# Placing small TensorE work later in a hand-planned instruction order: convolutional attention and correlation layers on one core

## The chip, the cores and the metric

The kernel runs on one NeuronCore of a Trainium2 chip. The metric is the device time in microseconds (us) of one execution. The core has five engines with a queue each: TensorE (PE in the profile; its weight loads are PEld), VectorE (DVE), ScalarE (ACT), GpSimd (POOL) and SyncE (SP), which here issues nearly all DMA transfers. SBUF is the on-chip memory, PSUM the memory that TensorE writes to.

## What is computed

Eight images of 768 channels and 32 x 32 pixels (1024 tokens) pass two residual layers. A group norm (32 groups) stands ahead of each. The first layer is an attention with 12 heads of 64 channels whose scores are outer products of variances; the second multiplies the pixels by a matrix, together with 28 local correlations of the pixel-normalized features.

```python
# layer 0: x = x + L0(gn(x))
q, k, v = qkv                                   # q is not used
var_v = var(v, axis=-1, ddof=1); var_k = var(k, axis=-1, ddof=1)
attn = softmax(var_v @ var_k.T * hd ** -0.5)    # 1024 x 1024 for each head
out = (attn @ v) @ W_proj.T + b_proj
# layer 1: x = x + L1(gn(x))
feat_n = feature / norm(feature, over channels)
corr[r, c] = sum over channels of shift(feat_n, r, c) * feat_n   # 28 shifts
out = concat(feature, corr) @ conv_w.T + conv_b
```

## The kernel before, in words

**Tiles.** An image is held as 128 partitions x 6 channel blocks x 1024 tokens in float32. A pair is two heads, so there are 6 pairs; a half is three pairs. Token tiles `t` are 128 tokens, 8 to an image; `hf` is a half of 512 tokens.

**Layer 0.** `Layer0.group(half, t)` multiplies a token tile by the key or the value weights of a half (six matmuls into one PSUM buffer of `mm`, which has 3). VectorE takes the statistics of each head from PSUM (line 307), values are copied to SBUF by ScalarE or VectorE, and after the eighth tile `head_m2` works out the squared deviations `m2`. For values, `spread` then transposes `m2` on TensorE (`to_rows`, line 279, tile `ptv`) and writes it as rows to DRAM. For keys, the maximum over all tokens is subtracted first (`nk`, with GpSimd's all-reduce, line 334), and the transpose is `ptk`. `Pair.rows` (line 382) reads a row back broadcast over 128 partitions: `bc` for the exponentials, `bk` for the denominators.

**Attention.** For each pair and each key tile ScalarE makes two tiles of exponentials (`exponentials`, line 392), and `products` multiplies them with the values (line 416, tile `av`). A step is one key tile. The denominators are a second pass of ScalarE over exponentials whose outputs are thrown away (`junk`, line 402) but whose sums are kept. After a pair's eighth denominator tile, `invert` takes the reciprocal on VectorE (line 425), `spread` transposes it on TensorE (line 431, tile `it`), writes it to DRAM (`di`) and reads it back broadcast (`rd`), and `finish` multiplies `av` by `rd` on VectorE (line 445). There are 6 buffers of exponentials (three steps), 2 of `av` and one of `rd`.

**Projection and layer 1.** `Project` multiplies the pairs' outputs by `wp` and adds to `x1` (lines 516, 525), where the image was loaded a second time. `Corr.gram(t)` multiplies a token tile with its neighbours (line 542) and VectorE picks 13 diagonals from the PSUM tile (line 550). After four grams `scale` works out the norms, `columns` applies them, `to_dram` transposes (line 577, tile `ct`) and writes rows; after eight, `gather` reads shifted rows for one half of the pixels and `product` multiplies them to `cs` (line 605). `Conv.group(n)` is the main product of an output block (line 630). If `cs` is ready, one more matmul adds the correlations (line 620, `cv<-cs`); if not, the unit leaves a late unit behind, `Conv.late`: the matmul `cc` into another PSUM buffer and an addition on VectorE (line 647). When all parts of a half are there, the half is stored; when all of both are, the next image's `x1` is loaded 12 us later.

**What sets the order.** Nothing is scheduled by the compiler: each engine executes its instructions in the order in which this program emits them. The program keeps a model clock (`Clock`). A unit of TensorE work is emitted and the clock is advanced by the unit's assumed time: 3.9 us for a key or value group, 2.4 for a gram, 5.2 for a conv, 0.9 for a late product. `later.after(us, job)` puts a job on a list; it is emitted when the clock passes its due time, which may be in the middle of a unit's or step's time, and so behind that unit's instructions. A second model time, `clock.act`, follows ScalarE: `EXP` and `SUM` are its assumed times for one exponential and one denominator tile, `STEP_US` TensorE's for one step of `products`. `work_off` alternates: if `can_run` says that ScalarE is far enough, four steps are emitted (a run; 12 runs to an image), otherwise the first unit of the list `rest` whose gate is ready (`pick`). If no more than `TAIL` us of other work is left, it is held back until the attention is over. The list of image `b` holds the second half of its values, layer 1 of image `b - 1` and all keys of image `b + 1`. The last value group also starts the load of the next image, and 14 us later `first_norm`: twelve statistics on VectorE, then `means` (TensorE tile `pma`), `spreads` (`pva`) and `apply`.

Of the kernel before, what the change touches and what calls it, by code (L numbers as in the profile page):

```python
# [32 lines left out]
HH = NH // 2  # L33
STEPS = 4
AHEAD = 3
TAIL = 8.0
EXP, SUM, STEP_US = 1.12, 1.32, 1.78


def windows(ap, *dims):  # L40
# [48 lines left out]
def two_layers(ctx, tc, x, wkv, wproj, bproj, wconv, wcorr, bconv, out):  # L89
# [26 lines left out]
    clock = Clock()  # L116
    later = clock
    ready = set()
# [7 lines left out]
    def small(name):  # L126
        return smp.tile([P, 512], F32, tag="sm", name=name)
# [5 lines left out]
    def load(pl, tag, b):  # L133
        t = pl.tile([P, J, N], F32, tag=tag, name=f"{tag}{b}")
        for j in range(J):
            nc.sync.dma_start(out=t[:, j, :], in_=xv[b, :, j, :])
        return t
# [30 lines left out]
    xn = load(xnpool, "xn", 0)  # L168
# [43 lines left out]
    def gn_tile(name):  # L212
        return st.tile([P, 2 * J, 6], F32, tag="bn", bufs=2, name=name)

    def gn_stats(bn, t, j, hf):
        nc.vector.bn_stats(out=bn[:, 2 * j + hf, :], in_=t[:, j, hf * HF : (hf + 1) * HF])  # L216
# [30 lines left out]
            for j in range(J):  # L247
                nc.vector.tensor_scalar(to[:, j, :], src[:, j, :], self.mean, self.rstd, ALU.subtract, ALU.mult)  # L248

    def first_norm(b, xn):  # L250

        bn = gn_tile(f"bn1_{b}")
        for j in range(J):
            for hf in range(2):
                gn_stats(bn, xn, j, hf)
        norm = Norm(bn, f"a{b}")
        later.after(3.0, norm.means)
        later.after(6.0, norm.spreads)

        def apply():  # L260
            norm.apply(xn, xn)
            ready.add(("xn", b))

        later.after(8.0, apply)


    def head_m2(bn, m2, name):
# [17 lines left out]
    class Layer0:  # L285
# [31 lines left out]
        def to_dram(self, cols, half):  # L317
            to_rows(cols, self.dr[half], f"{self.kind}{self.b}_{half}")
            ready.add((self.kind, self.b, half))

    class Keys(Layer0):
# [7 lines left out]
        def spread(self, half):  # L329
            b, m2 = self.b, self.m2[half]  # L330
            top = st.tile([P, HH], F32, tag="top", name=f"top{b}_{half}")
            nc.vector.tensor_reduce(top, m2.rearrange("p t h -> p h t"), AX.X, ALU.max)
            most = st.tile([P, HH], F32, tag="most", name=f"most{b}_{half}")
            nc.gpsimd.partition_all_reduce(most, top, P, bass_isa.ReduceOp.max)
            nk = st.tile([P, MT, HH], F32, tag="nk", bufs=4, name=f"nk{b}_{half}")
            self.nk.append(nk)

            def scaled():
                for t in range(MT):
                    nc.vector.tensor_tensor(nk[:, t, :], m2[:, t, :], most, ALU.subtract)  # L340
                nc.vector.tensor_scalar(nk, nk, HD ** -0.5 / (HD - 1) ** 2, None, ALU.mult)
                later.after(2.0, lambda: self.to_dram(nk, half))

            later.after(2.0, scaled)

    class Values(Layer0):
# [11 lines left out]
                    nc.vector.tensor_copy(to, at)  # L358

        def spread(self, half):  # L360
            later.after(2.5, lambda: self.to_dram(self.m2[half], half))


    class Pair:
        def __init__(self, b, hp, keys, values, ot):
            half = hp // 3
            self.b, self.hp, self.half, self.vt, self.ot = b, hp, half, values.vt[hp], ot
            self.keys, self.values = keys, values
            self.rows_at = {}
            self.exs = {}  # L370
            self.passes = {"e": 0, "s": 0}

# [37 lines left out]
        def products(self, t):  # L410
            if t == 0:
                self.av = avp.tile([P, 2, HF], F32, tag="av", name=f"av{self.b}_{self.hp}")
            exs = self.exs.pop(t)
            for hf in range(2):
                for e in range(2):
                    nc.tensor.matmul(  # L416
                        self.av[e * HD : (e + 1) * HD, hf, :], lhsT=self.vt[:, t, e, :],
                        rhs=exs[e][:, hf * HF : (hf + 1) * HF], start=t == 0, stop=t == MT - 1,
                    )
            if t == MT - 1:  # L420
                later.after(1.0, self.finish)

        def invert(self):
            self.inv = st.tile([P, 2 * MT], F32, tag="inv", bufs=2, name=f"inv{self.b}_{self.hp}")
            nc.vector.reciprocal(self.inv, self.sums.rearrange("p e t -> p (e t)"))
            later.after(1.5, self.spread)

        def spread(self):
            b, hp = self.b, self.hp
            pt = small(f"it{b}_{hp}")  # L430
            nc.tensor.transpose(pt[0 : 2 * MT, 0:P], self.inv, ident)
            row = work([2 * MT, P], f"ir{b}_{hp}")
            nc.vector.tensor_copy(row, pt[0 : 2 * MT, 0:P])
            dr = dpool.tile([2 * MT, P], F32, tag="inv", name=f"di{b}_{hp}")
            nc.sync.dma_start(out=dr, in_=row)
            self.rd = rdpool.tile([P, N], F32, tag="rd", name=f"rd{b}_{hp}")
            for e in range(2):
                nc.sync.dma_start(
                    out=self.rd[e * HD : (e + 1) * HD, :], in_=windows(dr[e * MT : e * MT + 1, :], (0, HD), (1, N))
                )  # L440

        def finish(self):
            for hf in range(2):
# [87 lines left out]
    class Corr:  # L531
# [25 lines left out]
        def scale(self, hf, dd):  # L557

            b = self.b
            m = st.tile([P, 4], F32, tag="m", name=f"m{b}_{hf}")  # L560
            nc.vector.tensor_scalar(m, dd[:, :, 0], NORM_EPS2, None, ALU.max)
            rn = st.tile([P, 4], F32, tag="rn", name=f"rn{b}_{hf}")
            nc.gpsimd.tensor_tensor(rn, m, neghalf, ALU.pow)

            def columns():
                dn = st.tile([P, 4, NROW], F32, tag="dn", bufs=2, name=f"dn{b}_{hf}")
                nc.vector.tensor_copy(dn[:, :, 0], rn)
                nc.vector.tensor_tensor(dn[:, :, 13], dd[:, :, 0], rn, ALU.mult)
                for q in range(4):
                    nc.vector.scalar_tensor_tensor(  # L570
                        dn[:, q, 1:13], dd[:, q, 1:13], rn[:, q : q + 1], mask_m, ALU.mult, ALU.mult
                    )
                later.after(3.0, lambda: to_dram(dn))

            def to_dram(dn):
                pt = small(f"ct{b}_{hf}")
                nc.tensor.transpose(pt[0 : 4 * NROW, 0:P], dn.rearrange("p q r -> p (q r)"), ident)
                cr = work([4 * NROW, P], f"cr{b}_{hf}")
                nc.vector.tensor_copy(cr, pt[0 : 4 * NROW, 0:P])
                for q in range(4):  # L580
                    at = PAD + hf * HF + q * P
                    nc.sync.dma_start(out=rows[b % 2][:, at : at + P], in_=cr[q * NROW : (q + 1) * NROW, :])
                if hf == 1:
                    self.gather()

            later.after(2.5, columns)
# [88 lines left out]
    def do(unit):  # L675

        more = unit[2]()
        clock.pass_time(unit[0])
        return [more] if more else []

    def pick(rest):
        n = next((n for n, r in enumerate(rest) if r[1] is None or r[1] in ready), None)
        return None if n is None else rest.pop(n)

    def work_off(rest, attention=None):
        while rest or (attention and not attention.over()):
            if attention and not attention.over():
                attention.load_rows()
                clock.feed_act()
                if attention.can_run():  # L690
                    attention.run()
                    continue
                if sum(r[0] for r in rest) <= TAIL:
                    clock.pass_time(0.5)
                    continue
            unit = pick(rest)
            if unit is None:
                clock.pass_time(0.5)
            else:
                rest[:0] = do(unit)  # L700

    first_norm(0, xn)
    clock.settle()
    x1s = [load(x1pool, "x1", 0)]
    keys, values = Keys(0, xn), Values(0, xn)
# [3 lines left out]
    for b in range(NB + 1):  # L709
        rest, attention = [], None  # L710
# [10 lines left out]
        if b + 1 < NB:  # L721

            def next_image(b=b):
                t = load(xnpool, "xn", b + 1)
                next_keys.xn = t
                clock.after(14.0, lambda: first_norm(b + 1, t))

            next_keys = Keys(b + 1, None)
            last = next(n for n, r in enumerate(rest) if n + 1 == MT * (1 + (b == 0)))
            us, gate, unit = rest[last]  # L730
            rest[last] = (us, gate, always(lambda unit=unit: (unit(), next_image())))
            rest += layer0_units(next_keys, (0, 1), ("xn", b + 1))
        work_off(rest, attention)
        if b < NB:
# [14 lines left out]
            norm = Norm(project.bn, f"b{b}")  # L749
# [45 lines left out]
```

## Time and profile before

The median of three runs is 3330.92 us (3329.41 to 3335.73). The profiled execution spans 3330.4 us.

| engine | busy, us | share | instructions |
|---|---|---|---|
| PE | 3011.1 | 90% | 9568 |
| ACT | 1794.3 | 54% | 2497 |
| DVE | 1072.9 | 32% | 4689 |
| POOL | 37.1 | 1% | 73 |

The costliest groups on PE are `av` (734.9 us), the convs (512.1), keys (511.1), values (505.8) and the projection (525.9 in two groups). The mean granted TensorE clock is 0.961 of full speed. Images 1 to 6 take some 400 us each and look alike.

How to read the lines below: a line of the timeline has start, duration, engine, source line, operation, output <- inputs, shapes and count, then in brackets the idle time of the engine before it and what it waited for. A line of the waits has the waiting instruction, what released it, the idle time in all, the number of waits and the longest. Float32 matmuls show as two records each. An idle time of an engine that is not the bottleneck costs nothing.

### The profile page before, as it was taken

To read this page: it belongs to the slowest core of one execution; us is meant where nothing else is said; L and a number is where in the kernel's file an instruction comes from. 1 tells how busy PE (TensorE), PEld (TensorE's weight loads), DVE (VectorE), ACT (ScalarE), POOL (GpSimd) and SP (SyncE) were. 2 spreads that over 40 slices of the span, in tenths; PEclk is the share of its full clock that TensorE was granted. 3 is DMA by queue.
4 is the path that set the end of the run, shared out by engine and by line. 5 is a ranking of instruction groups with operands and counts; after the bars stand their busy time and mean duration, and the time that the engine had idled before them with its cause. 6 is when DMAs were issued, how large, how long until landed. Compare 5 with 4: busy or idle time off the path is not lost.

```text
span 3330.4 us, 28877 instructions
## 1 busy us (share of the span) xinstructions
PE 3011.1 (90%) x9568; PEld 1439.0 (43%) x9568; DVE 1072.9 (32%) x4689; ACT 1794.3 (54%) x2497; POOL 37.1 (1%) x73
## 2 busy tenths in 40 slices
PE   7978798899988998999989999889998899997698
PEld 4433354344543444434444445434454344542244
DVE  3231135312352234422344123441235312342044
ACT  0669326781467805776058740777326782377700
POOL 0000000000000000000000000000000000000000
PEclk9988899999999999999999999999999999999799
DMA  3231113231232213142031411324113231222201
GB/s 134 99 126 56 35 67 112 73 136 36 81 116 84 107 64 118 52 141 76 37 137 44 160 55 54 111 68 155 35 67 112 73 136 35 74 86 86 73 39 42
DMA packets 86606, 282.29 MB, mean 85 GB/s; under 512 B 12702, under 2 KB 15902, under 8 KB 84410
## 3 DMA queue, kind: packets, MB, share of 16 engines
q1 hardware_dynamic: 84730, 275.74, 23.9%
q10 hardware_dynamic: 1728, 4.72, 0.4%
q8 instruction: 75, 1.23, 0.2%
q14 instruction: 73, 0.60, 0.1%
HBM read 253.59 MB, written 26.83 MB: 84 GB/s over the span
## 4 chain that ended last, share of the span: by engine, by line
PE 84%; DVE 5%; ACT 5%; DMA 4%; issue 1%; SPq 1%; POOL 0%; ACTq 0%; DVEq 0%; POOLq 0%
PE av L416 17%; PE k L301 15%; PE v L301 15%; PE pr L516 14%; PE cv L630 14%; PE gr L542 4%; ACT junk L402 3%; PE cc L620 2%; ACT ex L392 2%; DVE bn L216 1%; DMA di<-ir 1%; DMA rd<-di 1%; DVE sc L550 1%; PE cv L620 1%; DVE vbn L307 0%
## 5 line engine op out<-in xcount | busy, mean ns | idle before, releaser
L392 ACT ACTIVATE ex<-bc,nk 128x1024 f32<-128x1024 f32 x768 | 812.3, 1135 | 521.6 <-PE av L416 438.0
L402 ACT ACTIVATE junk<-bk,m2v 128x1024 bf16<-128x1024 f32 x768 | 880.3, 1146 | 38.6 <-DMA bk<-drk 16.8
L416 PE MATMUL av<-ex,v 128*64 128x512 f32 x3072 | 734.9, 627 | 29.6 <-ACT ex L392 29.6
L301 PE MATMUL k<-wk,xn 128*128 128x384 f32 x1536 | 511.1, 492 | 3.7 <-DVE xn L248 1.8
L630 PE MATMUL cv<-f,wc 128*128 128x512 f32 x1152 | 512.1, 594 | 0.0
L301 PE MATMUL v<-wv,xn 128*128 128x384 f32 x1536 | 505.8, 489 | 0.0
L356 ACT COPY v<-v 128x128 f32<-128x128 f32 x192 | 38.6, 274 | 765.9 <-PE v L301 765.9
L416 PEld LDWEIGHTS av<-ex,v 128*64 128x64 f32 x3072 | 224.9, 143 | 478.3 <-issue 413.8
L516 PE MATMUL pr<-v,wp 128*128 128x512 f32 x960 | 427.7, 592 | 0.0
L301 PEld LDWEIGHTS k<-wk,xn 128*128 128x128 f32 x1536 | 291.0, 191 | 229.5 <-issue 34.9
L301 PEld LDWEIGHTS v<-wv,xn 128*128 128x128 f32 x1536 | 290.3, 191 | 204.7 <-issue 12.3
L630 PEld LDWEIGHTS cv<-f,wc 128*128 128x128 f32 x1152 | 217.1, 191 | 245.0 <-issue 244.7
L550 DVE CUSTOM_DVE_ANT_0 sc<-gr,ident 128x128 f32<-128x128 f32 x832 | 242.1, 291 | 135.5 <-PE gr L542 108.6
L516 PEld LDWEIGHTS pr<-v,wp 128*128 128x128 f32 x960 | 182.5, 190 | 229.5 <-issue 229.5
L307 DVE BATCH_NORM_STATS2 kbn<-k 128x6 f32<-128x64 f32 x768 | 112.4, 218 | 392.0 <-PE k L301 391.9
L525 DVE SCALAR_TENSOR_TENSOR x<-pr,bproj_sb,x 128x512 f32<-128x512 f32 x96 | 71.8, 748 | 334.7 <-PE pr L516 319.5
L307 DVE BATCH_NORM_STATS2 vbn<-v 128x6 f32<-128x64 f32 x768 | 113.0, 217 | 155.1 <-ACT v L356 155.1
L445 DVE TENSOR_TENSOR v<-av,rd 128x512 f32<-128x512 f32 x80 | 51.6, 686 | 342.0 <-DMA rd<-di 326.7
L636 DVE SCALAR_TENSOR_TENSOR x<-cv,bconv_sb,x 128x512 f32<-128x512 f32 x96 | 72.0, 750 | 273.9 <-PE cv L620 176.2
L542 PE MATMUL gr<-f 128*128 128x227 f32 (+1 forms) x768 | 154.6, 352 | 1.7 <-DVE f L248 1.7
L542 PEld LDWEIGHTS gr<-f 128*128 128x128 f32 x768 | 138.4, 193 | 33.4 <-issue 29.0
L402 ACT ACTIVATION_READ_ACCUMULATOR junk<-bk,m2v 128x1 f32 x768 | 143.2, 186 | 0.0
(81 smaller groups left out, 886.5 us busy)
## 6 DMA issues: line engine op xcount, KB each, us to landing
bc<-drv SPq DMA_DIRECT2D x96, 512.0 KB
bk<-drk SPq DMA_DIRECT2D x96, 512.0 KB
xn<-in_x_dram SPq DMA_DIRECT2D x48, 512.0 KB
x<-in_x_dram SPq DMA_DIRECT2D x48, 512.0 KB
rd<-di SPq DMA_DIRECT2D x96, 256.0 KB
out_dram<-x SPq DMA_DIRECT2D x16, 1536.0 KB
wp<-in_wproj_dram SPq DMA_DIRECT2D x8, 2304.0 KB
wc<-in_wconv_dram SPq DMA_DIRECT2D x8, 2304.0 KB
```

Of the source, the lines that this page charges most:

```text
L301: nc.tensor.matmul(ps, lhsT=self.xn[:, j, t * P : (t + 1) * P], rhs=self.w[:, j, half * 384 : half * 384 + 384], start=j == 0, stop=j == J ...
L307: nc.vector.bn_stats(out=self.bn[:, t * HH + h, :], in_=ps[:, h * HD : (h + 1) * HD])
L392: nc.scalar.activation(ex, self.bc[e], AF.Exp, scale=self.keys.nk[self.half][:, t, h : h + 1])
L402: nc.scalar.activation(junk, self.bk[e], AF.Exp, scale=self.values.m2[self.half][:, t, h : h + 1], accum_out=self.sums[:, e, t : t + 1],)
L416: nc.tensor.matmul(self.av[e * HD : (e + 1) * HD, hf, :], lhsT=self.vt[:, t, e, :], rhs=exs[e][:, hf * HF : (hf + 1) * HF], start=t == 0, ...
L516: nc.tensor.matmul(self.ps[n], lhsT=self.w[:, hp, i, :], rhs=self.ots[hp][:, hf * HF : (hf + 1) * HF], start=hp == 0, stop=hp == HP - 1,)
L525: nc.vector.scalar_tensor_tensor(to, self.ps.pop(n), bproj_sb[:, i : i + 1], to, ALU.add, ALU.add)
L542: nc.tensor.matmul(ps[:, :n], lhsT=f[:, j, t * P : (t + 1) * P], rhs=f[:, j, t * P : t * P + n], start=j == 0, stop=j == J - 1,)
L550: nc.vector.tensor_tensor_reduce(out=sc, in0=ps[:, o : o + P], in1=ident, scale=1.0, scalar=0.0, op0=ALU.mult, op1=ALU.add, accum_out=self ...
L620: nc.tensor.matmul(ps, lhsT=wcorr_sb[:, n % J, :], rhs=cs[:, n // J, :], start=start, stop=True)
L630: nc.tensor.matmul(ps, lhsT=self.w[:, j, i, :], rhs=self.f[:, j, at], start=j == 0, stop=j == J - 1 and not joined)
L636: nc.vector.scalar_tensor_tensor(to, ps, bconv_sb[:, i : i + 1], to, ALU.add, ALU.add)
```

## The change

Only the order of the emitted instructions changes; no instruction is added or removed.

- Delays ahead of small TensorE work become longer: the transposes of values, of keys, of the inverse denominators and of the correlation columns, and the two matmuls of `first_norm`. The purpose is that the transposed data is ready when TensorE gets there.
- `finish` is placed only when both the pair's last products and its inverse's transpose are emitted, and no sooner than 6.5 us of model time after the latter (`try_finish`), so that VectorE need not stand waiting for `rd`.
- `pick` prefers a large unit after a small one, so that late correlation products don't follow each other.
- The model durations become 1.08, 1.28 and 1.92 us in place of 1.12, 1.32 and 1.78, and `TAIL` 13 us in place of 8.

```diff
@@ -33,8 +33,8 @@
 HH = NH // 2
 STEPS = 4
 AHEAD = 3
-TAIL = 8.0
-EXP, SUM, STEP_US = 1.12, 1.32, 1.78
+TAIL = 13.0
+EXP, SUM, STEP_US = 1.08, 1.28, 1.92
 
 
 def windows(ap, *dims):
@@ -247,21 +247,21 @@
             for j in range(J):
                 nc.vector.tensor_scalar(to[:, j, :], src[:, j, :], self.mean, self.rstd, ALU.subtract, ALU.mult)
 
-    def first_norm(b, xn):
+    def first_norm(b, xn, wait):
 
         bn = gn_tile(f"bn1_{b}")
         for j in range(J):
             for hf in range(2):
                 gn_stats(bn, xn, j, hf)
         norm = Norm(bn, f"a{b}")
-        later.after(3.0, norm.means)
-        later.after(6.0, norm.spreads)
+        later.after(wait, norm.means)
+        later.after(wait + 4.0, norm.spreads)
 
         def apply():
             norm.apply(xn, xn)
             ready.add(("xn", b))
 
-        later.after(8.0, apply)
+        later.after(wait + 6.0, apply)
 
 
     def head_m2(bn, m2, name):
@@ -339,7 +339,7 @@
                 for t in range(MT):
                     nc.vector.tensor_tensor(nk[:, t, :], m2[:, t, :], most, ALU.subtract)
                 nc.vector.tensor_scalar(nk, nk, HD ** -0.5 / (HD - 1) ** 2, None, ALU.mult)
-                later.after(2.0, lambda: self.to_dram(nk, half))
+                later.after(5.0, lambda: self.to_dram(nk, half))
 
             later.after(2.0, scaled)
 
@@ -358,7 +358,7 @@
                     nc.vector.tensor_copy(to, at)
 
         def spread(self, half):
-            later.after(2.5, lambda: self.to_dram(self.m2[half], half))
+            later.after(5.0, lambda: self.to_dram(self.m2[half], half))
 
 
     class Pair:
@@ -367,6 +367,7 @@
             self.b, self.hp, self.half, self.vt, self.ot = b, hp, half, values.vt[hp], ot
             self.keys, self.values = keys, values
             self.rows_at = {}
+            self.over, self.spread_at = False, None
             self.exs = {}
             self.passes = {"e": 0, "s": 0}
 
@@ -418,15 +419,18 @@
                         rhs=exs[e][:, hf * HF : (hf + 1) * HF], start=t == 0, stop=t == MT - 1,
                     )
             if t == MT - 1:
-                later.after(1.0, self.finish)
+                self.over = True
+                self.try_finish()
 
         def invert(self):
             self.inv = st.tile([P, 2 * MT], F32, tag="inv", bufs=2, name=f"inv{self.b}_{self.hp}")
             nc.vector.reciprocal(self.inv, self.sums.rearrange("p e t -> p (e t)"))
-            later.after(1.5, self.spread)
+            later.after(4.0, self.spread)
 
         def spread(self):
             b, hp = self.b, self.hp
+            self.spread_at = clock.now
+            self.try_finish()
             pt = small(f"it{b}_{hp}")
             nc.tensor.transpose(pt[0 : 2 * MT, 0:P], self.inv, ident)
             row = work([2 * MT, P], f"ir{b}_{hp}")
@@ -438,6 +442,11 @@
                 nc.sync.dma_start(
                     out=self.rd[e * HD : (e + 1) * HD, :], in_=windows(dr[e * MT : e * MT + 1, :], (0, HD), (1, N))
                 )
+
+        def try_finish(self):
+
+            if self.over and self.spread_at is not None:
+                later.after(max(STEP_US + 1.0, self.spread_at + 6.5 - clock.now), self.finish)
 
         def finish(self):
             for hf in range(2):
@@ -570,7 +579,7 @@
                     nc.vector.scalar_tensor_tensor(
                         dn[:, q, 1:13], dd[:, q, 1:13], rn[:, q : q + 1], mask_m, ALU.mult, ALU.mult
                     )
-                later.after(3.0, lambda: to_dram(dn))
+                later.after(5.0, lambda: to_dram(dn))
 
             def to_dram(dn):
                 pt = small(f"ct{b}_{hf}")
@@ -678,28 +687,33 @@
         clock.pass_time(unit[0])
         return [more] if more else []
 
-    def pick(rest):
-        n = next((n for n, r in enumerate(rest) if r[1] is None or r[1] in ready), None)
-        return None if n is None else rest.pop(n)
+    def pick(rest, last):
+
+        can = [n for n, r in enumerate(rest) if r[1] is None or r[1] in ready]
+        other = [n for n in can if rest[n][0] > 1.0 or last > 1.0]
+        return rest.pop((other or can)[0]) if can else None
 
     def work_off(rest, attention=None):
+        last = 9.0
         while rest or (attention and not attention.over()):
             if attention and not attention.over():
                 attention.load_rows()
                 clock.feed_act()
                 if attention.can_run():
                     attention.run()
+                    last = 9.0
                     continue
                 if sum(r[0] for r in rest) <= TAIL:
                     clock.pass_time(0.5)
                     continue
-            unit = pick(rest)
+            unit = pick(rest, last)
             if unit is None:
                 clock.pass_time(0.5)
             else:
+                last = unit[0]
                 rest[:0] = do(unit)
 
-    first_norm(0, xn)
+    first_norm(0, xn, 1.0)
     clock.settle()
     x1s = [load(x1pool, "x1", 0)]
     keys, values = Keys(0, xn), Values(0, xn)
@@ -723,7 +737,7 @@
             def next_image(b=b):
                 t = load(xnpool, "xn", b + 1)
                 next_keys.xn = t
-                clock.after(14.0, lambda: first_norm(b + 1, t))
+                clock.after(14.0, lambda: first_norm(b + 1, t, 10.0))
 
             next_keys = Keys(b + 1, None)
             last = next(n for n, r in enumerate(rest) if n + 1 == MT * (1 + (b == 0)))
```

## The prediction

> **What bounds the kernel now.** I read the page first (busy time and the chain), then the waits of PE, then the timeline of one middle image (480 to 880 us), then the timelines of the first and the last attention, where another engine sets the pace. From the page, busy time and the chain that ended last:
>
> ```profile
> PE 3011.1 (90%) x9568; PEld 1439.0 (43%) x9568; DVE 1072.9 (32%) x4689; ACT 1794.3 (54%) x2497; POOL 37.1 (1%) x73
> PE 84%; DVE 5%; ACT 5%; DMA 4%; issue 1%; SPq 1%; POOL 0%; ACTq 0%; DVEq 0%; POOLq 0%
> ```
>
> TensorE is the bound, and an edit that only reorders can win no more than its idle time, 3330.4 - 3011.1 = 319 us, and what matmuls lose to a lower clock after idling. Who PE waited for (us in all, times, longest):
>
> ```profile
> PE it L431 <- DVE inv L425: 95.5, 15, 9.1
> PE cc L620 <- DVE x L647: 51.7, 7, 8.0
> PE ptv L279 <- DVE m2v L274: 38.1, 16, 2.4
> PE av L416 <- ACT ex L392: 29.6, 4, 8.4
> PE pma L229 <- DVE mva L224: 28.1, 2, 19.4
> PE ct L577 <- DVE dn L570: 24.8, 16, 1.6
> PE ptk L279 <- DVE nk L341: 10.0, 6, 1.7
> ```
>
> These are nearly all the idle time, and all but `av` are the small transposes and products that the change moves. How they lie in one image, PE's timeline:
>
> ```profile
> 523.02 3.66 PE L416 MATMUL av<-ex,v 128*64 128x512 f32 x16
> 535.24 0.38 PE L431 MATMUL it<-ident,inv 128*16 128x128 f32 x1 [8.56 <-DVE inv L425]
> 536.51 5.29 PE L416 MATMUL av<-ex,v 128*64 128x512 f32 x16
> ...
> 639.83 8.30 PE L620 MATMUL cc<-cs,wcorr_sb 128*128 128x512 f32 x12 [7.26 <-DVE x L647]
> ```
>
> and VectorE's at the same two places:
>
> ```profile
> 527.35 7.21 DVE L216 BATCH_NORM_STATS2 bn<-xn 128x6 f32<-128x512 f32 x12
> 534.60 0.48 DVE L224 BATCH_NORM_AGGREGATE mva<-bn 128x2 f32<-128x72 f32 x1
> 534.99 0.20 DVE L425 RECIPROCAL inv<-sums 128x16 f32<-128x16 f32 x1
> ...
> 637.89 1.29 DVE L445 TENSOR_TENSOR v<-av,rd 128x512 f32<-128x512 f32 x2 [8.23 <-DMA rd<-di]
> ```
>
> So the 8.56 us is a reciprocal queued behind twelve statistics of the next image, and the 7.26 us is a correlation product out of PSUM buffers, because VectorE stood in `finish` waiting for a row transfer. The same sixteen `av` records take 3.66 us before the first gap and 5.29 after it.
>
> [...] 5.29 against 3.66 us above; twelve `cc` in 8.30 us where 12 x 0.43 = 5.2 is the usual pace. [...] So a long gap costs its length and 2 to 3 us more, and where VectorE's instructions stand matters as much as when PE asks.
>
> **The change, part by part.** I followed the planner's clock by hand through one image. With the old numbers this gives the order of the trace (seven value groups, a run of four `av` steps, a value group, gram, conv, gram, a run with `it` after two steps), so I trust it for the new ones. It puts the runs after the same units up to the correlation: the new ACT model per run, 4 x 2 x (1.08 + 1.28) = 18.9 us, is about the 18.5 that ACT takes in the trace (8.3 + 10.2), where the old one says 19.5.
>
> *Value transposes (2.5 to 5.0).* A group is 3.9 us in the model. Due at +2.5, `ptv` stands right behind its own group and waits for copy, statistics and m2: 2.40 and 2.36 us in every image. At +5.0 it stands behind the next value group (3.88 us) or the next gram (2.3 us), which hide it. Won: 4.7 an image. Added: the row loads `bc` are asked for one group later. Behind them are ACT's first exponentials, ready (6.3 + 10.2 us later) still about when the first run starts, so nothing is lost.
>
> *Key transposes (2 + 5).* `ptk` goes behind two `av` steps in place of one where the 1.66 us wait shows (0.38 more for the `it` behind it). In the new order the eighth group has another key group behind it, which hides it as well. Won: 2.0 an image, and 1.7 us of slow clock in about half of them (24 `av` in 7.07 in place of 5.37 us): 2.9.
>
> *Inverse (1.5 to 4.0).* For pair 0 the reciprocal is due at T+15.1 (T: start of the last value group), `first_norm` at T+14.0; before it was 15.3. The statistics therefore still stand ahead, and the reciprocal ends at the same moment. `it` goes behind three steps of the run in place of two: the gap is 8.56 - 1.76 = 6.8 us[...]. Won: 1.7, and 0.37 for `pma`, which moves behind a conv: 2.0. The other five pairs have no gap in middle images, and the new one hides nothing there.
>
> *Correlation columns (3 to 5).* Gram and conv are 2.4 + 5.2 = 7.6. `ct` was due at 2.5 + 3 = 5.5, now at 7.5: both inside the conv's time, so it stands behind the same conv and in front of the same gram. Its 1.55 us waits stay. Won: 0.
>
> *`try_finish` and `pick`.* `finish` is now at least 6.5 us after `it`; in the trace the rows land 6.8 us after it (582.3 to 589.1), 12.4 in the correlation stretch. There it now stands behind a conv's eviction, and the nine late products are no longer in one block: one late, conv, one late, conv, run, and so on among key groups. Three PSUM buffers are enough for that while VectorE waits. Won: 7.26 us and 3.1 of slow clock, less 0.3 more on `cs`: 10.0. Price: the next image's `x1` load moves one run later in the order, far enough ahead of its use, but now right ahead of the last pair's `bk` rows on the DMA queue. [...] ACT may wait 3 to 4 us, and PE then 0 to 3 (not in the trace of before): I take 1.5.
>
> Middle images 1 to 6: 4.7 + 2.9 + 2.0 + 10.0 - 1.5 = 18.1 each, **109 us**.
>
> *Image 0* has too little other work and ends when ACT ends. ACT's idle there is 4.3 + 6.3 + 7.6 + 12.3 + 5.6 + 4.2 = 40.4 us. The 12.3 is PE standing in `pma` (8.71) and `pva` (10.13) in front of a run that was ready; with `wait` 10 the run comes between them, leaving 3.6. The 7.6 is `bk` behind the `drv` writes, which now go after it, leaving 1 to 2. Three key groups between runs in place of four at times take most of 4.3, 5.6 and 4.2; about 5 stays of the 6.3. That leaves 12: 28 won, less some 3 for a third held key group (TAIL 13): **25**.
>
> *Image 7*: also ACT's. Its idle is 37.4, 13.1 of it at the correlation block; by the same steps some 18 stay. Won 19. But seven late products and the last conv (7 x 0.9 + 5.2 = 11.5) are now under TAIL and held till the end: 7 x 0.86 = 6 us on the path, and `x1` can't be loaded before the last of them, 1 to 2 more: **11**.
>
> *Last layer*: conv 9 fills the waits on `cs` (2.56 + 1.37, and 1.9 slow): **5**. `first_norm(0)` at 1.0 changes no order: nothing else is placed between.
>
> Sum: 109 + 25 + 11 + 5 = 150; 3330.9 - 150 = **3181 us**.
>
> **The rivals.** *The waits only change names* (0.14): `finish` still blocks VectorE with PSUM full, the held work eats what images 0 and 7 win. Then only the transposes count: 16 x 2.3 + 12 + 5 + 10 for image 0 = 63, so 3268. For it: the transfer takes 12.4 us where 6.5 are allowed. Against: the late products are thinned to one per conv.
> *More* (0.08): the reciprocal comes ahead of the statistics in some order that I mis-followed by 1.1 us, and 6.8 + 2.1 go as well: 6 x 8.9 = 53, so 3128.
> *Slower* (0.04): row loads that come later hold up ACT, 8 x 3.9 = 31, held work adds 3 + 6, and nothing is won: 3371. Against: ACT is 54% busy, and in middle images it waits for PE (438 us), not PE for it.
> *No change* (0.02): gains and losses cancel, 3331.
>
> **How the numbers follow.** The likeliest (0.72) gives 3181. Its own uncertainty: 5 us in each middle image (30), 12 for image 0, 7 for image 7; together some 35. The range of 3138 to 3242 leaves out most of the first and last rivals and half of the second. Faster: 0.72 + 0.14 + 0.08 = 0.94; same 0.02; slower 0.04.
>
> **What would show it.** Right: `ptv` and `ptk` below 5 us in PE's waits, `cc <- x L647` nearly gone, `it` still about 6.8 us once in each middle image, `ct` still 24.8 in all. The period of a middle image, 400 us now, about 382; PE busy about 2950 by less slow clock. Wrong: `ct` gone or `it` gone (the order was mis-followed), `av <- ex` grown beyond 40 us (ACT held up by rows), `finish` waiting above 5 us with `cc` or `k` waiting for VectorE.

## The result, and the profile after

The changed kernel takes 3181.94 us (median of four, 3180.45 to 3184.48) against 3331.61 before: a ratio of 0.955, with a 95% interval of 0.9534 to 0.9567. Predicted were 3181. PE has 9568 instructions and ACT 2497 in both. VectorE has two more than before: two more correlation products come late, and each brings an addition of its own (`x<-cc,x`, 74 in place of 72). So the 150 us are waits and what follows from them. From the page after, busy time and the chain that ended last:

```profile
PE 2978.2 (94%) x9568; PEld 1432.7 (45%) x9568; DVE 1071.9 (34%) x4691; ACT 1791.4 (56%) x2497; POOL 37.1 (1%) x73
PE 86%; ACT 4%; DMA 4%; DVE 3%; SPq 1%; issue 1%; POOL 0%; ACTq 0%; DVEq 0%; POOLq 0%
```

TensorE still sets the end. Its idle time fell from 319 to 3178.7 - 2978.2 = 200 us, and its busy time by 33 us for the same instructions, at a higher mean granted clock (0.977, before 0.961). In images 1 to 6 alone it is idle 72.6 us in place of 161.8 and busy 2210.4 in place of 2240.3. Who PE waited for after the change (us in all, times, longest):

```profile
PE it L435 <- DVE inv L427: 80.8, 11, 8.4
PE av L417 <- ACT ex L393: 28.1, 8, 9.1
PE pma L229 <- DVE mva L224: 26.3, 2, 19.4
PE ct L586 <- DVE dn L579: 24.8, 16, 1.6
PE cc L629 <- DVE cs L614: 17.0, 9, 2.4
PE pva L240 <- DVE ea L235: 3.4, 2, 2.7
PE pr L525 <- DVE x L534: 3.4, 1, 3.4
PE ptv L279 <- DVE m2v L274: 2.4, 1, 2.4
```

`cc <- x` (51.7 before) and `ptk` (10.0) are gone, `ptv` went from 38.1 to 2.4. `ct` has the same 24.8 us as before, `it` only 15 less. The two places of one image that were shown of before, on PE's timeline after:

```profile
496.24 5.37 PE L417 MATMUL av<-ex,v 128*64 128x512 f32 x24
508.45 0.38 PE L435 MATMUL it<-ident,inv 128*16 128x128 f32 x1 [6.85 <-DVE inv L427]
508.77 3.68 PE L417 MATMUL av<-ex,v 128*64 128x512 f32 x8
...
602.49 1.10 PE L629 MATMUL cc<-cs,wcorr_sb 128*128 128x512 f32 x2 [1.84 <-DVE cs L614]
603.42 5.31 PE L639 MATMUL cv<-f,wc 128*128 128x512 f32 x12
```

and on VectorE's:

```profile
500.56 7.21 DVE L216 BATCH_NORM_STATS2 bn<-xn 128x6 f32<-128x512 f32 x12
507.81 0.48 DVE L224 BATCH_NORM_AGGREGATE mva<-bn 128x2 f32<-128x72 f32 x1
508.20 0.19 DVE L427 RECIPROCAL inv<-sums 128x16 f32<-128x16 f32 x1
...
610.30 1.28 DVE L454 TENSOR_TENSOR v<-av,rd 128x512 f32<-128x512 f32 x2
```

The transpose now has three steps (24 records) ahead of it and waits 6.85 us in place of 8.56, since the reciprocal still stands behind the 7.21 us of statistics. The eight records behind that wait take 3.68 us at a mean granted clock of 0.50; the eight behind an `it` that does not wait (at 598.71 us) take 1.94 at 1.00. `finish` (line 454 now) starts without waiting for `rd`. ScalarE still waits 252.6 us for TensorE's `av` (438.0 before), and 102.9 us for the rows `bc` (83.2 before), but TensorE waits for ScalarE's exponentials only in images 0 and 7. So neither ScalarE nor the rows `bc` set the pace of the middle images; there TensorE waits only for `it`, `ct` and, some 2 us an image, `cs`.

Where the time went, by stretches that end with the first projection matmul of an image (from PE's timeline):

| stretch | before | after | won | predicted |
|---|---|---|---|---|
| start to projection of image 0 | 374.6 | 354.4 | 20.2 | 25 |
| images 1 to 6 | 2402.2 | 2283.1 | 119.1 | 109 |
| image 7 | 374.7 | 363.7 | 11.0 | 11 |
| from there to the end | 178.9 | 177.6 | 1.3 | 5 |

A middle image takes 380.5 us in place of 400.4.

### The profile page after: what moved, and what is told of

Same layout as the page of the kernel before. It is cut to its first block, busy times and chain, and to the rows that moved or that the text cites. A ratio compares the mean times of both kernels' runs of the same rounds, so it can differ in the third digit from the quotient of the medians.

```text
span 3178.7 us, 28882 instructions
## 1 busy us (share of the span) xinstructions
PE 2978.2 (94%) x9568; PEld 1432.7 (45%) x9568; DVE 1071.9 (34%) x4691; ACT 1791.4 (56%) x2497; POOL 37.1 (1%) x73
## 4 chain that ended last, share of the span: by engine, by line
PE 86%; ACT 4%; DMA 4%; DVE 3%; SPq 1%; issue 1%; POOL 0%; ACTq 0%; DVEq 0%; POOLq 0%
PE av L417 18%; PE k L301 16%; PE v L301 16%; PE pr L525 15%; PE cv L639 14%; PE gr L551 4%; ACT junk L403 2%; PE cc L629 2%; DMA bk<-drk 2%; ACT ex L393 2%; DVE bn L216 1%; PE cv L629 1%; DMA xn<-in_x_dram 1%; DMA wk<-in_wkv_dram 0%; DMA out_dram<-x 0%
## 5 line engine op out<-in xcount | busy, mean ns | idle before, releaser
L393 ACT ACTIVATE ex<-bc,nk 128x1024 f32<-128x1024 f32 x768 | 810.7, 1135 | 355.8 <-PE av L417 252.6
L358 DVE COPY v<-v 128x128 f32<-128x128 f32 x192 | 44.0, 285 | 208.4 <-PE v L301 208.4
```

The source lines that it names most:

```text
L393: nc.scalar.activation(ex, self.bc[e], AF.Exp, scale=self.keys.nk[self.half][:, t, h : h + 1])
```

## The experiments

My theory had three parts: TensorE is the bound, so a wait removed is time won; a wait is removed where the written order puts work between a small operation and what it needs; and each edit wins its own wait. The rivals: waits only change names; ScalarE or the row transfers set the pace; another part than the one I credit does the work. Each ratio is to the kernel before, with its 95% interval. The kernel before was timed anew beside each group of runs (medians of 3331.6 to 3335.5), so a difference of 3 or 4 us between runs of different groups says little. The edits are shown as excerpts; the comments in them are added here.

| run | what it is | us | ratio |
|---|---|---|---|
| changed kernel | | 3181.9 | 0.955 [0.9534, 0.9567] |
| a1_transposes | before, `ptv` and `ptk` delays alone | 3346.2 | 1.0031 [1.002, 1.0042] |
| a2_pick | before, new `pick` alone | 3317.5 | 0.9939 [0.9919, 0.996] |
| a3_finish | before, later `finish` alone | 3368.5 | 1.0097 [1.0082, 1.0112] |
| a4_model | before, new durations alone | 3340.1 | 1.0012 [1.0005, 1.0019] |
| u1_durations | changed, old durations | 3268.9 | 0.9809 [0.9794, 0.9823] |
| u2_pick | changed, old `pick` | 3181.8 | 0.9548 [0.9532, 0.9564] |
| u3_finish | changed, early `finish` | 3227.5 | 0.9689 [0.9674, 0.9704] |
| b1_stats_late | changed, statistics later | 3176.3 | 0.9526 [0.951, 0.9542] |
| b2_tail8 | changed, `TAIL` 8 | 3167.9 | 0.95 [0.9484, 0.9516] |
| b3_columns_late | changed, `ct` later | 3156.1 | 0.9468 [0.9454, 0.9482] |
| c1_all | b1, b2 and b3 together | 3136.5 | 0.9408 [0.9394, 0.9422] |
| c2_norm | c1 and first norm retimed | 3112.6 | 0.934 [0.9326, 0.9354] |

### One part alone: the waits change names

**a1_transposes**

```diff
-later.after(2.0, lambda: self.to_dram(nk, half))        # keys
+later.after(5.0, lambda: self.to_dram(nk, half))
-later.after(2.5, lambda: self.to_dram(self.m2[half], half))   # values
+later.after(5.0, lambda: self.to_dram(self.m2[half], half))
```

> The kernel before with only the longer delays of the value and key transposes (2.5 and 2.0 to 5.0). The values' rows are asked for later, and by that the first run comes one value group later; by the written order the inverse's transpose of pair 0 then stands behind a gram and two convs and not inside a run. Theory (TensorE is the bound; what counts is the waits that the order leaves): the value transposes fall from 2.4 to about 0.6 us, the 8.56 us wait on the reciprocal and its slow restart go too, the wait of the correlation products stays. 6 x (3.6 + 10.6 + 2) = 97, some 5 in images 0 and 7: about 3230. Rival (parts add up; each delay wins only its own wait): 6 x 7.6 + 5 = 50, so 3281.

Measured: 3346.2, a little slower than before. Both expectations miss. PE's timeline of a middle image of this kernel:

```profile
930.43 0.59 PE L229 MATMUL pma<-mva,group 128*128 128x1 f32 x2 [8.48 <-DVE mva L224]
...
946.88 0.38 PE L431 MATMUL it<-ident,inv 128*16 128x128 f32 x1 [5.34 <-DVE inv L425]
...
1152.93 10.52 PE L416 MATMUL av<-ex,v 128*64 128x512 f32 x48
1173.70 0.38 PE L431 MATMUL it<-ident,inv 128*16 128x128 f32 x1 [10.25 <-DVE inv L425]
```

and VectorE's at the second and the last line:

```profile
942.25 4.42 DVE L248 TENSOR_SCALAR xn<-xn,meana,rstda 128x1024 f32<-128x1024 f32 x6
946.58 0.24 DVE L425 RECIPROCAL inv<-sums 128x16 f32<-128x16 f32 x1
...
1173.39 0.25 DVE L425 RECIPROCAL inv<-sums 128x16 f32<-128x16 f32 x1 [19.47 <-ACT junk L402]
```

The expectations followed `it` alone. In the shifted order `pma`, at 3 us behind the statistics, waits for them in its place; the reciprocal stands behind `apply`; and at the image's end six steps come with nothing between, so the last pair's transpose waits 10.25 us for ScalarE's denominators. The value transposes' wait did nearly go (5.8 us in all of PE's waits, 38.1 before); what was won was lost elsewhere.

**a2_pick**: the new `pick(rest, last)` in the kernel before, all else old.

> The kernel before with only the new pick: late correlation products one at a time among larger units; finish stays where it was and still stands in VectorE's queue waiting for the rows. Theory (the 7.26 us is three PSUM buffers filled by small products while VectorE stands): larger units cover most of it, some 2 us stay, and the slow restart goes. 6 x 8 = 48 and some 7 in image 7: about 3276. Rival (the wait is VectorE's, so only finish placed later helps): the wait stays above 6 us and the time within 10 us of 3331.

Measured: 3317.5 (3308.8 to 3326.5), of the sign of the theory and about a third of its size. The block's wait of 7.26 us became 2.2, on a conv that waits for a PSUM buffer:

```profile
1038.17 1.02 PE L620 MATMUL cc<-cs,wcorr_sb 128*128 128x512 f32 x2
1041.42 7.09 PE L630 MATMUL cv<-f,wc 128*128 128x512 f32 x12 [2.22 <-DVE x L647]
```

The middle image is only 0.9 us shorter (399.5): by the waits of this kernel, a key group and the last pair's `it` now wait where they did not (`k <- x` 7.1 us in all, `it` 108.2 where before had 95.5). The rest of the gain lies in image 7 (4.5 us) and the last layer (2.6).

**a3_finish**

```diff
-                later.after(1.0, self.finish)
+                self.over = True
+                self.try_finish()       # max(STEP_US + 1.0, spread_at + 6.5 - now)
```

> The kernel before with only the later finish (6.5 us behind the inverse's transpose); late products still in one block. By the written order VectorE evicts two of the nine late products before it meets finish, whose rows land 12.4 us after the transpose. Theory: the block then stops after five products in place of three: the wait falls from 7.26 to about 4.5 us; 6 x 3 = 18 and a little in image 7: about 3310. Rival (finish placed later is what cured it): the wait is gone, 6 x 10 = 60, about 3270.

Measured: 3368.5, the slowest of all, with 5.8 us more in each middle image:

```profile
1047.09 6.40 PE L629 MATMUL cc<-cs,wcorr_sb 128*128 128x512 f32 x8 [5.72 <-DVE x L656]
...
1173.35 0.38 PE L435 MATMUL it<-ident,inv 128*16 128x128 f32 x1 [6.04 <-DVE inv L427]
```

The block stops after five products, as the theory said, and its wait shrinks, though to 5.72 us and not to 4.5. The loss is the second line: the last pair's transpose waits for a reciprocal that itself waits for ScalarE:

```profile
1173.04 0.25 DVE L427 RECIPROCAL inv<-sums 128x16 f32<-128x16 f32 x1 [8.39 <-ACT junk L403]
```

In this order four key groups stand between runs at several places where before has three, and only one is left ahead of the last. Why a later `finish` moves runs at all is in the code: each job's due time is also a moment at which the planner feeds ScalarE's list. That this alone is the reason was not tried.

**a4_model**

```diff
-EXP, SUM, STEP_US = 1.12, 1.32, 1.78
+EXP, SUM, STEP_US = 1.08, 1.28, 1.92
```

> The kernel before with only the model durations 1.08, 1.28 and 1.92. By the written order the first run comes one value group earlier, and pair 0's reciprocal and its transpose come ahead of the next image's statistics. Theory: the 8.56 us wait and its slow restart go, the other waits stay; 6 x 10.5 = 63 and some 5 in image 0: about 3263. Rival (better durations alone change little, since TensorE is busy anyway and the reciprocal waits for ScalarE's last denominators): within 15 us of 3331.

Measured: 3340.1. The reciprocal's wait of 8.56 us did go, as the theory said, but the 68 us expected of it did not come: a middle image takes 403.0 us. PE's and VectorE's timeline of one image:

```profile
1034.39 8.41 PE L620 MATMUL cc<-cs,wcorr_sb 128*128 128x512 f32 x12 [7.23 <-DVE x L647]
1091.35 5.80 PE L301 MATMUL k<-wk,xn 128*128 128x384 f32 x12 [4.12 <-DVE kbn L307]
```

```profile
1089.13 1.29 DVE L445 TENSOR_TENSOR v<-av,rd 128x512 f32<-128x512 f32 x2 [16.97 <-DMA rd<-di]
```

Here the last pair has its work, but `finish` still stands early: VectorE waits 17 us for `rd`, and a key group waits 4.12 us for PSUM. In a3 it is the other way round: `finish` stands late, and the last pair lacks its work. That these two edits need each other is what I take from this; the two without the rest were not run.

The four alone give +0.3, -0.6, +1.0 and +0.1%; together with the other delays and `TAIL` they give -4.5%. My third premise, that each edit wins its own wait, falls.

### One part undone: which part carries the gain

Undone were the durations, `pick` and the later `finish` (and `TAIL` below, in b2). The longer delays were not undone, so what they carry in the whole is not shown by a run; it is only read from the waits.

**u1_durations**: the changed kernel with 1.12, 1.32, 1.78.

> The changed kernel with the old model durations (1.12, 1.32, 1.78). By the written order the other work then runs out before the last two runs of each image, which stand together. Theory (durations set how much work is placed between runs; too much early leaves TensorE waiting for ScalarE at the end): av <- ex and it <- inv appear at the end of each middle image, some 11 us and a slow restart; against that the wait of pair 0's reciprocal shrinks, since it stands behind more work: 6 x 8 = 48, about 3235. Rival (the delays carry the gain, the durations are only closer to the trace): at most 3190.

Measured: 3268.9; 87 us of the 150 come back, more than I expected. Ends of the same middle image, first with the old durations, then the changed kernel:

```profile
714.62 5.37 PE L417 MATMUL av<-ex,v 128*64 128x512 f32 x24
720.84 9.21 PE L417 MATMUL av<-ex,v 128*64 128x512 f32 x32 [0.84 <-ACT ex L393]
738.44 0.38 PE L435 MATMUL it<-ident,inv 128*16 128x128 f32 x1 [8.40 <-DVE inv L427]
739.19 3.83 PE L417 MATMUL av<-ex,v 128*64 128x512 f32 x8 [0.37 <-ACT ex L393]
```

```profile
703.82 11.88 PE L301 MATMUL k<-wk,xn 128*128 128x384 f32 x36
715.62 5.37 PE L417 MATMUL av<-ex,v 128*64 128x512 f32 x24
720.92 0.28 PE L435 MATMUL it<-ident,inv 128*16 128x128 f32 x1
721.13 1.94 PE L417 MATMUL av<-ex,v 128*64 128x512 f32 x8
```

With the old durations the planner puts too much other work between early runs; the last two stand together and TensorE waits for ScalarE (32 records of `av` in 9.21 us, usually 7.09, then 8.40 of idling). Against that, pair 0's wait of 6.85 us is gone, as expected. A middle image takes 391.3 us, 10.8 more. By its waits, `it` has 1.6 us more than in the changed kernel, `av` 1.2, and `pma` and `pva` 3.5 that were not there; TensorE is also busy 3.7 us longer. So the end of the image is only a part of the loss.

**u2_pick**: the changed kernel with the old `pick`.

> The changed kernel with the old pick: nine late products in one block, all else in the same order up to there. finish now stands behind five of their evictions. Theory (either of the two edits is nearly enough for the 7.26 us wait, since each keeps VectorE from standing while the three buffers fill): 2 to 3 us a middle image come back, about 3197. Rival (spacing out is what cured it): the 10 us come back, 6 x 10 = 60, about 3242.

Measured: 3181.8, the same as the changed kernel and below both expectations. The nine late products are one block again (18 records), behind a wait for `cs` alone:

```profile
598.70 8.23 PE L629 MATMUL cc<-cs,wcorr_sb 128*128 128x512 f32 x18 [2.03 <-DVE cs L614]
```

Five are evicted before `finish`, whose rows have then landed:

```profile
603.88 1.28 DVE L454 TENSOR_TENSOR v<-av,rd 128x512 f32<-128x512 f32 x2
```

In the changed kernel, spacing out the products is worth next to nothing: a middle image is 0.4 us longer without it and the last layer 0.9. Image 0 is 3.5 us shorter, though TensorE's order is the same there, so that much is variation between runs.

**u3_finish**: the changed kernel with `finish` emitted as soon as it can be; TensorE's order is exactly the same.

```diff
-later.after(max(STEP_US + 1.0, self.spread_at + 6.5 - clock.now), self.finish)
+later.after(max(1.0, self.spread_at + 0.1 - clock.now), self.finish)
```

> The changed kernel with finish emitted as soon as the pair's last products and its transpose are out, not 6.5 us behind the transpose; TensorE's order is exactly the changed kernel's, only VectorE's differs. Theory (as for the old pick): VectorE stands waiting for rd again, over 150 us in all, but TensorE loses only 1 to 3 us an image, about 3195. Rival (finish placed later is what cured it): about 3242.

Measured: 3227.5, 46 us back, between the two expectations and nearer the rival's 3242, but not for the rival's reason. At the correlations nothing comes back: there the wait is for `cs`, as in the changed kernel. VectorE and PE some 100 us later in the same image:

```profile
704.96 1.29 DVE L454 TENSOR_TENSOR v<-av,rd 128x512 f32<-128x512 f32 x2 [8.99 <-DMA rd<-di]
```

```profile
665.47 4.14 PE L301 MATMUL k<-wk,xn 128*128 128x384 f32 x12 [1.60 <-DVE x L656]
709.65 0.41 PE L279 MATMUL ptk<-ident,nk 128*48 128x128 f32 x1 [4.18 <-DVE nk L341]
```

VectorE's waits for `rd` rose from 32.2 to 320.0 us in all. Most cost TensorE nothing; a key's transpose whose `nk` stands behind `finish` does. Image 0 is 10.6 us longer, since there the next image's statistics stand behind `finish`. VectorE's and PE's lines in image 0:

```profile
197.74 1.29 DVE L454 TENSOR_TENSOR v<-av,rd 128x512 f32<-128x512 f32 x2 [15.38 <-DMA rd<-di]
```

```profile
206.72 0.58 PE L229 MATMUL pma<-mva,group 128*128 128x1 f32 x2 [22.81 <-DVE mva L224]
```

This run and the one before it belong together. In the changed kernel either edit alone keeps the wait of 7.26 us away; the later `finish` is worth 46 us because of other instructions that would stand behind it on VectorE.

### What was left, and a better version

**b1_stats_late**: `clock.after(20.0, ...)` for `first_norm` in place of 14.0.

> The changed kernel with the next image's statistics 20 us after the last value group in place of 14, so that pair 0's reciprocal and the copy of its transpose stand ahead of them on VectorE. Theory (the remaining 6.85 us is the reciprocal behind 7.2 us of statistics, with 2 us of slow restart): both go in images 1 to 6, 6 x 8.9 = 53, a few us more in image 0: about 3127. Rival (the reciprocal waits for ScalarE's last denominators): the wait stays above 5 us and the time within 10 us of 3182.

Measured: 3176.3. The cause was right: `it <- inv` fell to 37.3 us, all in images 0 and 7. The gain was not: in image 0 `pma` waits longer and 3.7 us are lost, and in the middle images a wait took the place of the old one:

```profile
898.32 0.28 PE L229 MATMUL pma<-mva,group 128*128 128x1 f32 x2
903.19 0.59 PE L240 MATMUL pva<-ea,group 128*128 128x1 f32 x2 [4.59 <-DVE ea L235]
```

`pma` and `pva` now stand side by side with no other work between. The mean's copy stands on VectorE behind `finish`, which waits 4.10 us for `rd`, and behind the 13 diagonals of a gram and an eviction that `finish` has held up:

```profile
896.46 1.29 DVE L454 TENSOR_TENSOR o<-av,rd 128x512 f32<-128x512 f32 x2 [4.10 <-DMA rd<-di]
...
902.54 0.15 DVE L231 COPY meana<-pma 128x1 f32<-128x1 f32 x1
```

**b2_tail8**: `TAIL = 8.0`.

> The changed kernel with TAIL back at 8. Theory (held work lies on the path where ScalarE sets the pace, images 0 and 7): one key group less behind the attention of image 0 (3.9) and one late product with one conv less behind that of image 7 (6): 10 in all, about 3172; middle images unchanged at 380 us. Rival (TAIL 13 covers the last pair's inverse and its rows): waits of pr for VectorE in the middle images, slower than 3182.

Measured: 3167.9, 14 us won where 10 were expected; the middle images stay at 381.1, image 7 is 6.4 us shorter, image 0 5.6 (1.7 of these before the two orders part) and the last layer 3.6. In the changed kernel the larger `TAIL` is a loss.

**b3_columns_late**: `later.after(7.0, lambda: to_dram(dn))`.

> The changed kernel with the correlation columns' transpose at 7.0 in place of 5.0 behind columns, so past gram and conv (7.6 us). Theory (it stands behind the conv whose eviction precedes columns on VectorE): with another gram or conv between, the 16 waits of 1.55 us go: 25, less some 5 for correlations that come later: about 3162. Rival (the chain of columns is slower than the model thinks): the waits stay, and cs comes later, so 3182 to 3190.

Measured: 3156.1, 26 us won, of which some 3 lie in image 0, whose order the edit does not touch. `ct` is gone from PE's waits; `cc <- cs` rose by 5.2 us. So those waits were only a matter of 2 us of delay: at 5.0 the transpose stands behind the same conv as at 3.0.

**c1_all**

> All three of these together. Theory: the waits are in different places and add up: 55 + 10 + 20 = 85, about 3097. Rival (a later reciprocal, later rows and later correlations meet on the DMA queue, and new waits take the place of the old): above 3125.

Measured: 3136.5. The three alone win 5.7 + 14.0 + 25.9 = 45.6, together 45.5: here the parts add up to within what the runs vary. That they meet to 0.1 us is chance: b1's four runs alone span 10 us, and in single stretches the sum of the parts and the whole differ by up to 5 us.

**c2_norm**: c1 with `first_norm` retimed.

```diff
-clock.after(20.0, lambda: first_norm(b + 1, t, 10.0))
+clock.after(20.0 if b else 14.0, lambda: first_norm(b + 1, t, 16.0 if b else 10.0))
-later.after(wait + 4.0, norm.spreads)
+later.after(wait + 6.0, norm.spreads)
-later.after(wait + 6.0, apply)
+later.after(wait + 8.0, apply)
```

> The three edits together, and in images 1 to 6 the two small matmuls of first_norm later (16 and 22 us behind the statistics in place of 10 and 14), in image 0 the statistics back at 14. Theory (the new wait of pva, 4.6 to 5.7 us an image, is the mean's copy behind finish and evictions on VectorE): it goes with its slow restart, 6 x 6 = 36 and some 5 in image 0: about 3096. Rival (VectorE stands in finish anyway and hands the wait on): above 3125.

Measured: 3112.6, 6.6% faster than the kernel before (ratio 0.934) and the best here. `pva` is down to 1.9 us in all, a middle image takes 372.5. The rest of what was expected is a new wait of `ct` on middle images, whose columns now stand behind `apply`:

```profile
525.69 4.42 DVE L248 TENSOR_SCALAR xn<-xn,meana,rstda 128x1024 f32<-128x1024 f32 x6
```

```profile
531.54 0.30 PE L586 MATMUL ct<-ident,dn 128*56 128x128 f32 x1 [2.73 <-DVE dn L579]
```

## Why the prediction was right, and where it was not

- **The total** is within 1 us, which is better than its parts: middle images gave 10 us more than predicted, image 0 and the last layer 9 less. That these cancel is luck.
- **The order worked out by hand** was right. The trace after shows three steps ahead of `it`, one late product between convs, `ct` behind the same conv. The numbers that follow from it alone were right as well: `it` 6.85 us (6.8 predicted), `ct` 24.8 (24.8), `ptk` gone and `ptv` down to one wait of 2.4.
- **The price for `bk` behind the `x1` load** (1.5 us in each middle image, my estimate) was not paid: ScalarE's waits for `bk` are 4.0 us in all, in image 0. Against that the late products wait some 1.8 to 2.4 us for `cs`, where I had 0.3 more than before. The two nearly cancel. Most of the rest is slow clock: the mean granted clock of images 1 to 6 is 0.99 in place of 0.97, and a middle image's matmuls are busy 5.0 us less, where the terms of the sum held 4.0. The sign "PE busy about 2950" was missed (2978.2), but it did not follow from those terms: they come to some 26 us in all, so to 2985. The 438 us of ScalarE waiting for PE, which I gave for the middle images, are those of all eight; images 1 to 6 have 367.
- **Image 0**: of ScalarE's 40.4 us of idle time 12 were to stay; it is 16.6 (4.3, 0.7, 0.4, 4.0, 5.3 and three of 0.5 to 0.7), and its first exponential starts 2.2 us later than before. The terms that were mis-sized are the wait for `bk`, 4.0 in place of 1 to 2, and the gap behind the run that `pva` divides: 5.3, not nearly nothing, since four key groups and not three stand ahead of the next run. Much of the miss is variation, though: u2_pick and b3_columns_late have the same TensorE order in image 0 and take 350.8 and 351.2 us for it in place of 354.4, with 3.3 us in that gap.
- **The last layer**: "conv 9 fills the waits on `cs`" holds for one wait of 2.56 and not for the rest: two of 1.43 us stay. And `x1` comes later for image 7, as I said, 3.4 us of waiting in place of 1.4, but in this stretch.
- **The credit for the 7.26 us wait.** I put 10.0 us an image down to "`try_finish` and `pick`", and argued against the first rival that the late products are thinned out. The wait went, but the thinning was not needed for it: with the old `pick` (u2) it stays away, and so it does with the early `finish` (u3). In the kernel before neither edit alone was enough: 2.2 us stay with `pick`, 5.7 with `finish`. The 46 us that the later `finish` is worth lie elsewhere, and the sum shows nothing of them, since it compares the order before with the order after.
- **The durations had no term of their own.** I used them to place the runs and priced nothing. Undoing them costs 87 us, part of it because they also keep work for the end of each image. My sum hid this as well: both orders happen to have key groups ahead of the last run.
- **The rival "waits only change names"** was not this kernel's fate, but it is exactly what happens to three of its four parts alone. That the sum came out depended on pricing the whole new order, not the edits one by one.

## What to carry to other kernels

In an order written by a planner, price the whole new order and not the edits: a delay moves what comes after it, and a wait removed in one place returns on the next instruction whose input is late (in a1_transposes 8.48 us on `pma`). Look for the cause of a wait on the queue of the engine that was waited for: here it was work standing ahead of a short reciprocal (7.21 us of statistics ahead of 0.20), or an instruction that stands waiting for a transfer with others behind it (`finish`, 8.23 us for `rd`). A delay only counts when it passes the next unit of work; 3 to 5 us inside a stretch of 7.6 us of model time did nothing, 7 us won some 23 to 26.

## What the runs showed that I had not expected

The slow clock followed short gaps here too, and the same gaps did not always bring it. In the kernel before, all six middle images have a wait of 1.66 us and one of 0.38 behind it. In four of them the next 24 records take 7.07 us, in two 5.37:

```profile
722.89 0.29 PE L279 MATMUL ptk<-ident,nk 128*48 128x128 f32 x1 [1.66 <-DVE nk L341]
723.56 0.28 PE L431 MATMUL it<-ident,inv 128*16 128x128 f32 x1 [0.38 <-DVE rsk L281]
723.76 7.07 PE L416 MATMUL av<-ex,v 128*64 128x512 f32 x24
...
1123.99 5.37 PE L416 MATMUL av<-ex,v 128*64 128x512 f32 x24
```

The mean granted clock over these 24 records is 0.76 in the first case and 1.00 in the second. So in this kernel a gap's length alone does not tell what it costs. What else decides it was not tried.
